# Key tiles spread by transfers, attention output in even rows, and one transfer per gate tile

## The chip, the cores and the metric

The kernel runs on one core of a Trainium2 chip. The metric is the device time of one execution in microseconds (us), as the median of several runs. The core's engines are named as in the profile: PE (TensorE matmuls), PEld (its weight loads), DVE (VectorE), ACT (ScalarE), POOL (GpSimd) and SP (SyncE, which here issues nearly all transfers, one after the other from one queue).

## The reference

128 sequences of 64 tokens with 128 channels go through four blocks, each with a condition vector of a sequence (`cond`) and a context of 64 tokens of a sequence (`ctx`). All arithmetic is float32. Cut to what matters here:

```python
# block L0 (and, with other weights, L2)
sh_sa, sc_sa, g_sa, sh_ff, sc_ff, g_ff = split(silu(t_emb) @ adaln_w + adaln_b, 6)
xm = ln(x) * (1 + sc_sa) + sh_sa
x = x + g_sa * (attend(q, k, v of xm @ qkv_w + qkv_b) @ sa_proj_w + sa_proj_b)   # self-attention
x = x + attend(ln(x) @ q_w + q_b, k and v of ctx) @ ca_proj_w + ca_proj_b        # cross-attention
x = x + g_ff * mlp(ln(x) * (1 + sc_ff) + sh_ff)
# block L1: cross-attention from a modulated x to a modulated context
# block L3: a small mixture of three experts with a gate
def attend(q, k, v):            # 16 heads of 8 channels
    return softmax(q @ k.T / sqrt(8)) @ v
```

## The kernel before, in words

The 8,192 tokens are 16 groups of 8 sequences (512 tokens). All of `x` stays in the on-chip memory, as 16 tiles `x0` to `x15` of 128 tokens by 4 by 128 channels. Five attention layers follow each other: L0s and L0c (self and cross of block L0), then the MLP of L0, then L1c, L2s and L2c, then the MLP of L2, then block L3.

In an attention layer a group goes through the generator `prepare` (load of the context, statistics, normalizing, transposing, then `kT`, `kbd`, `qT`, `vbd`), the two halves of `scores`, `turned` and `weighted`, and the generator `finish`. The function `step` writes by hand the order in which every engine gets its work: two steps for each group, with `go(prep, i + d)` and `go(fin, i - d)` taking the next part of a later or an earlier group. The order on each queue is exactly the order in which these lines issue. No scheduler changes it. `turned` follows `scores` by one step, and `weighted` by two.

Scores are matmuls over 32 rows, which are the 8 channels of 4 heads. To keep the heads apart, the keys stand in a block-diagonal tile `kbd` of 128 rows by 4 by 512: plane `j` holds the keys of one head of each four, and zeros in the other rows. POOL makes the four planes with four multiplications of `kT` by a column of a 0/1 `mask` (L444); DVE does it for the first group. `kbd` is drawn new from a pool for each group.

The values stand in `vbd`, two tiles that are kept, cleared once, with a column of ones for the softmax's sums. `weighted` gives `o`: in each 32 rows, rows 0 to 15 are the outputs of two heads and rows 16 and 17 the sums. There are two column planes, so that a second set of rows 0 to 15 belongs at rows 16 to 31 of the first plane.

`finish` divides. Part 1 writes the sums to DRAM by two transfers (`sums`, L538), reads them back spread over 128 rows (`rc`, L542), and moves the second plane's rows by four transfers `o<-o` (L545). Part 2 takes the reciprocal on DVE (L547), writes it back (`recs`, L549), loads the gate tile in a self-attention layer (`gt`, two transfers, L278) and loads the reciprocals spread over the rows (`rb`, L554). Part 3 multiplies on POOL (`oT`, L557) and adds the bias to `x`. Part 4 is the projection `py` on PE (L563).

`gt` has the gate and the gated bias of each token's sequence: 128 rows by 4 by 256. It is read from a DRAM table with one row of 1 KB for each sequence; every row is repeated for 64 tokens. It is loaded once a group in L0s and L2s, and once a group (a turn) in the MLP of L2.

Of the kernel before, what the change touches and what calls it, by code (L numbers as in the profile page):

```python
# [9 lines left out]
F32 = mybir.dt.float32  # L10
AF = mybir.ActivationFunctionType
ALU = mybir.AluOpType
# [23 lines left out]
for _name, _n in _VECS:  # L36
# [15 lines left out]
}  # L52
_RAW = [
    "x", "cond_1024", "ctx_1024", *_WTS,
    "L0_xcond_ca_proj_b", "L1_xcond_bp", "L2_xcond_b_cproj", "L3_xcond_router_b", "L3_xcond_e_b2",
# [4 lines left out]
def tile_kernel(ctx: ExitStack, tc: tile.TileContext, a: dict, out: bass.AP):  # L60
# [5 lines left out]
    def const(shape, name):  # L66
        return cp.tile(shape, F32, tag=name, name=name)
# [8 lines left out]
    nc.sync.dma_start(cond, a["cond_1024"])  # L76
    vec_rows = const([_NVEC, P], "vec_rows")
    nc.scalar.dma_start(vec_rows, a["vecs"])
    mask = const([P, 4], "mask")
    nc.scalar.dma_start(mask, a["mask"])  # L80

    w = {}

    def load_weights(prefix, pool=cp):
        for name, (k, n) in _WTS.items():
            if name.startswith(prefix):
                t = pool.tile([P, k, n], F32, tag=name, name=name)
                src = a[name]
                if len(src.shape) == 3:
                    src = src.rearrange("e c n -> (e c) n")  # L90
                nc.sync.dma_start(t, src.rearrange("(k p) n -> p k n", p=P))
                w[name] = t

    xs = [const([P, TT, P], f"x{s}") for s in range(NST)]
# [23 lines left out]

    ident = const([P, P], "ident")
    make_identity(nc, ident)  # L120
    nhalf = const([P, TT], "nhalf")
    G.memset(nhalf, -0.5)

# [37 lines left out]
    def mm(name):  # L161
        return pools[1].tile([P, 512], F32, tag="mm", name=name)
# [4 lines left out]
        Places.ak.tile([P, NB, 8, 32], F32, tag=f"vbd{i}", name=f"vbd{i}", bufs=1) for i in range(2)  # L167
    ]

    def clear(t):  # L170
        G.memset(t, 0.0)
        G.memset(t[0:L, :, :, 16:17], 1.0)
        G.memset(t[L:P, :, :, 17:18], 1.0)


# [2 lines left out]
    condT = const([P, P], "condT")  # L178
    scT = const([P, P], "scT")
    mods = {}  # L180

    def col(name, i=0):
        r = _ROW[name] + i
        return vec[:, r : r + 1]
# [19 lines left out]

    def folded_column(wp, bp, bv, i):
        pb = mm("pb")
        T.matmul(pb[:, 0:1], w[wp][:, 0], col(bv, i), start=True, stop=True)
        t = const([P, 1], "pb_" + wp)
        V.tensor_add(t, pb[:, 0:1], col(bp))
        proj_bias[wp] = t  # L210
# [3 lines left out]
    def gate_table(wmod, wp, i=2, bias=None):  # L214

        table = dp.tile([P, 2, P], F32, tag="gate_" + wp, name="gate_" + wp)
        rows = const([P, 2, P], "gate_rows")
        gb = const([P, P], "gate_bias")
        V.tensor_scalar_mul(gb, mods[wmod][:, i, :], proj_bias[wp] if bias is None else bias)

        def second():
            pg = mm("pg")
            for q, src in enumerate((mods[wmod][:, i, :], gb)):
                T.transpose(pg[:, ts(q, P)], src, ident)
            V.tensor_copy(rows, pg[:, 0 : 2 * P].rearrange("p (i c) -> p i c", i=2))
            nc.sync.dma_start(table, rows)
            gates[wp] = table

        return second

    def folded_row(wp, bp, bv):
        bvs = const([P, P], "bvs")
        V.tensor_copy(bvs, col(bv, 1).broadcast_to([P, P]))

        def second():
            pb = mm("pb")
            T.matmul(pb[:, :P], bvs, w[wp][:, 0], start=True, stop=True)
            V.tensor_add(row_bias[bp], row_bias[bp], pb[:, :P])
            proj_bias[wp] = row_bias[bp]

        return second

    def condition():
        pc = mm("pc")
        T.transpose(pc[:, :P], cond, ident)
        V.tensor_copy(condT, pc[:, :P])
        S.activation(scT, pc[:, :P], AF.Silu)
        pv = mm("pv")
        T.transpose(pv[:, :_NVEC], vec_rows, ident[:_NVEC, :_NVEC])
        V.tensor_copy(vec, pv[:, :_NVEC])  # L250
        V.tensor_scalar_add(vec1, vec, 1.0)

    first_mods = modulations("L0_xcond_adaln_w", "L0_xcond_adaln_b", 6, (1, 4))
# [19 lines left out]
    def gate_tile(pool, s, wp):  # L273

        gt = pool.tile([P, TT, 2, P], F32, tag="gt", name="gt")
        for h in range(2):
            r = gates[wp].rearrange("(s t h) i c -> s h t (i c)", t=TT, h=2)[s, h]
            nc.sync.dma_start(  # L278
                gt[ts(h, L)].rearrange("p t i c -> p t (i c)"),
                r.unsqueeze(0).broadcast_to([L, TT, 2 * P]),  # L280
            )
        return gt

    later_tables = [
# [14 lines left out]
    def by_batch(t):  # L299
        return t.rearrange("p (b l) -> p b l", b=NB)  # L300
# [80 lines left out]

    turn = [0]

    ctxT = dp.tile([NST, P, NT], F32, tag="ctxT", name="ctxT")

    def prepare(pools, at):
# [52 lines left out]
        i = turn[0] % 2  # L439
        turn[0] += 1  # L440
        vbd = vbds[i]
        kbd = pool.tile([P, 4, NB, L], F32, tag="kbd", name="kbd")
        for j in range(4):
            (V if at.get("first") else G).tensor_scalar(  # L444
                kbd[:, j], by_batch(kT), mask[:, j : j + 1], 1.0, ALU.mult, ALU.mult
            )
        yield
        pq = psum.tile([P, 512], F32, tag="mm", name="pq")
        T.matmul(pq, at["wq"], q_in, start=True, stop=True)  # L449
# [11 lines left out]
                    start=True, stop=True,  # L461
                )
        pv4 = pvv.rearrange("p b (i d) -> p b i d", d=HD)
        S.copy(vbd[0:L, :, :, 0:HD], pv4[0:L])
        S.copy(vbd[L:P, :, :, HD : 2 * HD], pv4[L:P])
        at["vbd"] = vbd

    def scores(pools, at, u):
# [61 lines left out]
    def finish(pools, at):  # L530

        pool, psum = pools[:2]
        s, o = at["s"], at["o"]
        cross = at["layer"][2] == "c"

        sums = dp.tile([16, NT], F32, tag="sums", name="sums", bufs=2)
        for j in range(2):
            nc.sync.dma_start(  # L538
                sums.rearrange("(g i j) t -> j g i t", i=2, j=2)[j], o[16 + j : P : 32, :, :]
            )  # L540
        rc = pool.tile([P, L], F32, tag="rc", name="rc")
        nc.sync.dma_start(rc, sums.rearrange("h (c t) -> (h c) t", t=L))  # L542

        for g in range(4):
            nc.sync.dma_start(o[32 * g + 16 : 32 * g + 32, 0, :], o[32 * g : 32 * g + 16, 1, :])  # L545
        yield
        V.reciprocal(rc, rc)  # L547
        recs = dp.tile([16, NT], F32, tag="recs", name="recs", bufs=2)
        nc.sync.dma_start(recs.rearrange("h (c t) -> (h c) t", t=L), rc)  # L549

        if not cross:
            gt = gate_tile(pool, s, at["wp"])
        rb = pool.tile([P, NT], F32, tag="rb", name="rb", bufs=1)
        nc.sync.dma_start(rb, recs.unsqueeze(1).broadcast_to([16, HD, NT]))  # L554
        yield
        oT = pool.tile([P, NT], F32, tag="oT", name="oT", bufs=1)
        G.tensor_tensor(oT, o[:, 0, :], rb, ALU.mult)  # L557
        bias = proj_bias[at["wp"]].unsqueeze(1).broadcast_to([P, TT, P]) if cross else gt[:, :, 1, :]
        G.tensor_tensor(xs[s], xs[s], bias, ALU.add)
        yield  # L560
        py = psum.tile([P, TT, P], F32, tag="mm", name="py")
        for t in range(TT):
            T.matmul(py[:, t, :], oT[:, ts(t, P)], w[at["wp"]][:, 0], start=True, stop=True)  # L563
        if cross:
            V.tensor_add(xs[s], xs[s], py)
        else:
            y = pool.tile([P, TT, P], F32, tag="y", name="y")
            V.tensor_tensor(y, py, gt[:, :, 0, :], ALU.mult)
            G.tensor_tensor(xs[s], xs[s], y, ALU.add)

    def attend(pools, ats):
# [5 lines left out]
        def go(gens, i):  # L577
            if 0 <= i < n:
                next(gens[i], None)
# [8 lines left out]
        def step(k, between=(), late=()):  # L588
# [11 lines left out]
            if past:  # L600
                weighted(pools, past["at"], past["u"], past["eT"])
            if u == 0:
                go(fin, i - 2)
                go(prep, i + 4)
                go(prep, i + 1)
                go(fin, i - 3)
            else:
                go(prep, i + 1)
# [16 lines left out]
    def attention_of(s, layer):  # L625
        if layer[2] == "s":
            wmod, wqkv, bqkv, wp = {
                "L0s": ("L0_xcond_adaln_w", "L0_xcond_qkv_w", "L0_xcond_qkv_b", "L0_xcond_sa_proj_w"),
                "L2s": ("L2_xcond_W_mod", "L2_xcond_W_qkv", "L2_xcond_b_qkv", "L2_xcond_W_proj"),
            }[layer]  # L630
            m = w[wqkv][:, 0]
            return dict(
                s=s, layer=layer, wmod=wmod, wp=wp, wq=m[:, 0:P], bq=col(bqkv, 0),
                wk=m[:, P : 2 * P], bk=col(bqkv, 1), wv=m[:, 2 * P : 3 * P],
            )
        wq, bq, wkv, bkv, wp = {
            "L0c": (
# [8 lines left out]
        }[layer]  # L646
        m = w[wkv][:, 0]
        return dict(
            s=s, layer=layer, wp=wp, wq=w[wq][:, 0], bq=col(bq), wk=m[:, 0:P], bk=col(bkv, 0),
            wv=m[:, P : 2 * P],  # L650
        )

# [537 lines left out]
    def stages():  # L1190
# [41 lines left out]
        clear(vbds[0])  # L1232
        ahead_1(0, 1, 2, 3)
        condition()
        ahead_1(0, 0)
        first_mods[0]()
        ahead_1(0, 0, 1, 2, 0, 0, 1)
# [11 lines left out]
            f()  # L1249
        first_mods[2]()  # L1250
        n = last + 2 + len(heads_0)
        for f in steps_1[6:-n]:
            f()
        for s in range(2):
            heads_0[3 + s] = lambda s=s, f=heads_0[3 + s]: (f(), load_context(s))
        rest = into_mlp(steps_1, heads_0, turns_0)
# [68 lines left out]
```

## Time and profile before

| what | value |
|---|---|
| median of 3 runs | 1628.25 us (1627.0 to 1634.33) |
| the profiled execution, its own time | 1626.31 us |
| its span, from the first instruction to the last | 1624.5 us |
| mean granted TensorE clock | 0.997 of full speed |
| POOL busy | 1072.5 us (66%) |
| time of all transfer packets on the main queue | 26.1% of 16 transfer engines' span |
| L0s, between starts of a group's first score reduction | 11.9 to 13.3 us |
| transfers that SP issues for a group in L0s | 11: `sums` 2, `rc` 1, `o` 4, `recs` 1, `gt` 2, `rb` 1 |

Busy times are of one profiled execution. In a line of the timeline the columns are the start, the time, the engine, the source line, the operation, what it writes and reads, and how often; in square brackets is how long the engine had stood idle before it, and what ended that. In a line of waits they are who waited, for whom, the sum in us, how often, and the longest. `SPq` is SP's queue: an issue there is not the transfer itself, which goes on after it.

### The profile page before, as it was taken

The page shows a single profiled execution, that of the slowest core. Times are in us where ns is not written, and L with a number is a line of the kernel's source. Part 1 is how long each engine was busy: PE and PEld are TensorE (multiplying, and loading weights), DVE is VectorE, ACT ScalarE, POOL GpSimd, SP SyncE. Part 2 cuts the span into 40 slices and gives each one's busy share as a digit, 9 for nine tenths or more (in the row PEclk, how much of TensorE's full clock was granted, in tenths as well). Part 3 has the DMA queues.
Part 4 walks back from the last instruction along what each step waited for, and adds up shares of the span by engine and source line. Part 5 has one row for each costly group of instructions (what it writes and reads, how often), then busy time and mean ns, then how long its engine had stood idle before and what let it go on. Part 6 is the DMA issues. An engine that isn't in the chain of part 4 may idle for free.

```text
span 1624.5 us, 64028 instructions
## 1 busy us (share of the span) xinstructions
PE 1573.8 (97%) x27842; PEld 1086.8 (67%) x27842; DVE 1240.4 (76%) x1566; ACT 1035.5 (64%) x1710; POOL 1072.5 (66%) x1786
## 2 busy tenths in 40 slices
PE   6999999998999899999999999998999999999998
PEld 4676777776544577776777777776777566666665
DVE  7898998898555688899899889896443566666666
ACT  5788777776433678878888888886334544444443
POOL 6687787766888789887787876775875333333322
PEclk9999999999999999999999999999999999999999
DMA  8334453332111022211334432222533111111100
GB/s 209 85 82 99 107 127 92 83 83 72 55 36 55 16 63 61 72 44 50 90 82 102 104 88 73 62 56 59 130 81 76 31 39 37 40 33 36 34 12 19
DMA packets 146775, 112.65 MB, mean 69 GB/s; under 512 B 36357, under 2 KB 125247, under 8 KB 146495
## 3 DMA queue, kind: packets, MB, share of 16 engines
q1 hardware_dynamic: 146288, 108.53, 26.1%
q8 instruction: 219, 3.59, 0.9%
q14 instruction: 61, 0.50, 0.1%
q10 hardware_dynamic: 207, 0.03, 0.0%
HBM read 83.99 MB, written 14.02 MB: 60 GB/s over the span
## 4 chain that ended last, share of the span: by engine, by line
PE 83%; DVE 12%; ACT 3%; issue 1%; DMA 0%; SPq 0%; DVEq 0%
PE sc L478 10%; PE pp L503 9%; PE po L520 7%; PE ph L693 7%; PE ph L1080 6%; PE ph L1081 6%; DVE e L487 6%; DVE mx L485 6%; PE po L1111 5%; PE psT L342 5%; PE pk L436 5%; PE py L563 4%; PE py L709 4%; PE py L699 3%; PE pvv L459 3%; PE pq L449 3%
## 5 line engine op out<-in xcount | busy, mean ns | idle before, releaser
L507 ACT ACTIVATE eT<-pp 128x1024 f32<-128x1024 f32 x320 | 329.7, 1030 | 160.8 <-PE pp L503 160.7
L485 DVE TENSOR_REDUCE mx<-sc 128x32 f32<-128x2048 f32 x160 | 366.6, 2291 | 83.6 <-PE sc L478 83.6
L487 DVE TENSOR_TENSOR e<-sc,mx 128x2048 f32<-128x2048 f32 x160 | 366.6, 2291 | 5.4
L503 PEld LDWEIGHTS pp<-ident,e 64*128 64x128 f32 x5120 | 183.9, 138 | 140.1 <-ACT eT L507 44.7
L503 PE MATMUL pp<-ident,e 64*128 64x64 f32 x5120 | 227.7, 229 | 7.2 <-DVE e L487 4.7
L444 POOL TENSOR_SCALAR kbd<-kT,mask 128x512 f32<-128x512 f32 x316 | 212.4, 690 | 31.3 <-ACT kT L438 28.3
L372 POOL TENSOR_SCALAR xn<-x,nmu,rs 128x128 f32<-128x128 f32 x508 | 223.6, 453 | 13.3
L557 POOL TENSOR_TENSOR oT<-o,rb 128x512 f32<-128x512 f32 x80 | 102.1, 1276 | 163.5 <-DMA rb<-recs 62.9
L478 PE MATMUL sc<-kbd,qT 32*64 32x256 f32 x5120 | 179.2, 387 | 16.6 <-DVE e L487 15.6
L694 ACT ACTIVATE h<-ph,vec 128x512 f32<-128x512 f32 x128 | 87.3, 687 | 149.9 <-PE ph L693 149.7
L520 PE MATMUL po<-eT,vbd 128*32 128x64 f32 x10240 | 178.1, 221 | 1.4 <-issue 1.3
L1087 ACT ACTIVATE h<-h 128x512 f32<-128x512 f32 x112 | 70.6, 630 | 149.8 <-DVE h L1083 130.9
L520 PEld LDWEIGHTS po<-eT,vbd 128*32 128x32 f32 x10240 | 151.3, 110 | 14.4 <-issue 2.0
L330 POOL TENSOR_TENSOR rs<-rs,nhalf 128x4 f32<-128x4 f32 x128 | 130.2, 1017 | 10.7
L478 PEld LDWEIGHTS sc<-kbd,qT 32*64 32x64 f32 x5120 | 97.7, 131 | 53.0 <-issue 19.6
L1083 DVE TENSOR_TENSOR h<-ph,ab 128x512 f32<-128x512 f32 x112 | 76.9, 687 | 62.6 <-PE ph L1081 62.5
L1116 DVE SCALAR_TENSOR_TENSOR acc<-po,pr,acc 128x128 f32<-128x128 f32 x192 | 67.2, 350 | 44.1 <-PE po L1111 39.6
L1080 PE MATMUL ph<-nx,w 128*128 128x512 f32 x192 | 100.7, 607 | 0.0
L528 ACT COPY o<-po 128x512 f32<-128x512 f32 x160 | 95.7, 598 | 5.1 <-PE po L520 2.0
L1081 PE MATMUL ph<-u,w_ev 128*128 128x512 f32 x192 | 98.9, 597 | 0.0
L1111 PEld LDWEIGHTS po<-w_2o,h 128*128 128x128 f32 x768 | 92.1, 192 | 8.7 <-issue 8.4
L1104 POOL TENSOR_SCALAR g<-g 128x512 f32<-128x512 f32 x16 | 9.9, 622 | 132.1 <-ACT g L1103 132.1
(259 smaller groups left out, 2868.5 us busy)
## 6 DMA issues: line engine op xcount, KB each, us to landing
rb<-recs SPq DMA_DIRECT2D x80, 256.0 KB
c<-in_ctx_dram SPq DMA_DIRECT2D x64, 256.0 KB
o<-o SPq DMA_DIRECT2D x320, 32.0 KB
gt<-gate_L_xcond_sa_proj_w SPq DMA_DIRECT2D x32, 256.0 KB
gt<-gate_L_xcond_W_proj SPq DMA_DIRECT2D x32, 256.0 KB
gt<-gate_L_xcond_W_mlp SPq DMA_DIRECT2D x32, 256.0 KB
x<-in_x_dram SPq DMA_DIRECT2D x16, 256.0 KB
ctxT<-cm SPq DMA_DIRECT2D x16, 256.0 KB
```

The source lines that it names most:

```text
L330: G.tensor_tensor(rs, rs, nhalf, ALU.pow)
L372: engine.tensor_scalar(xn[:, t, :], src[:, t, :], nmu[:, t : t + 1], rs[:, t : t + 1], ALU.add, ALU.mult)
L444: (V if at.get("first") else G).tensor_scalar(kbd[:, j], by_batch(kT), mask[:, j : j + 1], 1.0, ALU.mult, ALU.mult)
L478: T.matmul(sc[ts(h, L), g, ts(t2, 256)], qT[ts(g, 32), ts(b, L)], kbd[ts(g, 32), :, b, :], start=True, stop=True,)
L485: V.tensor_reduce(mx, sc.rearrange("p g (m k) -> p (g m) k", k=L), AX.X, ALU.max)
L487: V.tensor_tensor(e, sc.rearrange("p g (m k) -> p (g m) k", k=L), mx.unsqueeze(2).broadcast_to([P, 32, L]), ALU.subtract,)
L503: T.transpose(pp[:, h, ts(4 * g2 + 2 * i + t2, L)], e6[ts(h, L), 2 * gg + g2, t2, i], ident[ts(h, L), ts(h, L)],)
L507: S.activation(eT[:, gg], pp, AF.Exp, scale=HD ** -0.5)
L520: T.matmul(po[ts(g, 32), i, ts(2 * t2 + h, L)], at["vbd"][:, 4 * u + 2 * t2 + h, 2 * g + i, :], e7[:, g // 2, h, g % 2, i, t2, :], start=T ...
L1080: T.matmul(ps, wn, d["nx"], start=True, stop=False)
L1081: T.matmul(ps, we, d["u"], start=False, stop=True)
L1111: T.matmul(po[:, ex, :], d[q][:, ts(t, P)], k3["w_2o"][:, q, :], start=r == 0, stop=r == 1)
```

## The change

Four things are changed together.

1. The columns of the query and key weights are put in another order at run time (`reorder`), so that the rows of `kT` that belong to plane `j` are rows `j, j+4, j+8, ...`. Two `kbd` tiles are kept. The first two groups still fill them by the mask, which also writes the zeros; from the third group on, four transfers (`spread`) write only the key rows. `mask` is computed from the identity matrix.
2. The columns of `vbd` are laid out so that outputs stand in the even rows of `o` and sums in two odd rows. One transfer gives `sums`, one moves the second plane into the odd rows. The five projection weights are loaded with their rows in the matching order, by two transfers each, and `rb` is loaded by two transfers.
3. The gate table in DRAM is ordered so that the rows of a half of a group stand together, 4 KB, and `gt` is one transfer.
4. In `step`, `go(prep, i + 1)` (with the keys' transfers) stands ahead of `go(fin, i - 2)` (with `recs`). `finish` has one part more: `recs` is issued ahead of the context's load, `gt` and `rb` after it.

```diff
+    kbds = [
+        Places.ak.tile([P, 4, NB, L], F32, tag=f"kbd{i}", name=f"kbd{i}", bufs=1) for i in range(2)
+    ]
     def clear(t):
         G.memset(t, 0.0)
-        G.memset(t[0:L, :, :, 16:17], 1.0)
+        G.memset(t[0:L, :, :, 1:2], 1.0)
...
+    def reorder(engine, name, n):
+        for i in range(n):
+            t = const([P, P], "gate_bias")
+            cols = w[name][:, 0, ts(i, P)]
+            engine.tensor_copy(t.rearrange("p (g d j) -> p g d j", d=HD, j=4), by_element(cols))
+            engine.tensor_copy(cols, t)
...
         gt = pool.tile([P, TT, 2, P], F32, tag="gt", name="gt")
-        for h in range(2):
-            r = gates[wp].rearrange("(s t h) i c -> s h t (i c)", t=TT, h=2)[s, h]
-            nc.sync.dma_start(
-                gt[ts(h, L)].rearrange("p t i c -> p t (i c)"),
-                r.unsqueeze(0).broadcast_to([L, TT, 2 * P]),
-            )
+        r = gates[wp].rearrange("(s h t) i c -> s h (t i c)", t=TT, h=2)[s]
+        nc.sync.dma_start(
+            gt.rearrange("p t i c -> p (t i c)"),
+            r.unsqueeze(1).broadcast_to([2, L, TT * 2 * P]),
+        )
...
+    def spread(kbd, kT):
+        for j in range(4):
+            nc.sync.dma_start(kbd[j:P:4, j].rearrange("p b l -> p (b l)"), kT[j:P:4, :])
...
-        kbd = pool.tile([P, 4, NB, L], F32, tag="kbd", name="kbd")
-        for j in range(4):
-            (V if at.get("first") else G).tensor_scalar(
-                kbd[:, j], by_batch(kT), mask[:, j : j + 1], 1.0, ALU.mult, ALU.mult
-            )
+        kbd = kbds[i]
+        by_mask = turn[0] <= 2
+        if by_mask:
...
+        else:
+            spread(kbd, kT)
...
-        S.copy(vbd[0:L, :, :, 0:HD], pv4[0:L])
-        S.copy(vbd[L:P, :, :, HD : 2 * HD], pv4[L:P])
+        S.copy(vbd[0:L, :, :, 0 : 2 * HD : 2], pv4[0:L])
+        S.copy(vbd[L:P, :, :, 2 * HD : 4 * HD : 2], pv4[L:P])
...
-        for j in range(2):
-            nc.sync.dma_start(
-                sums.rearrange("(g i j) t -> j g i t", i=2, j=2)[j], o[16 + j : P : 32, :, :]
-            )
+        nc.sync.dma_start(sums.rearrange("(m i) t -> m i t", i=2), o[1:P:16, :, :])
...
-        for g in range(4):
-            nc.sync.dma_start(o[32 * g + 16 : 32 * g + 32, 0, :], o[32 * g : 32 * g + 16, 1, :])
+        nc.sync.dma_start(o[1:P:2, 0, :], o[0:P:2, 1, :])
         yield
         V.reciprocal(rc, rc)
         recs = dp.tile([16, NT], F32, tag="recs", name="recs", bufs=2)
         nc.sync.dma_start(recs.rearrange("h (c t) -> (h c) t", t=L), rc)
+        yield
         if not cross:
             gt = gate_tile(pool, s, at["wp"])
         rb = pool.tile([P, NT], F32, tag="rb", name="rb", bufs=1)
-        nc.sync.dma_start(rb, recs.unsqueeze(1).broadcast_to([16, HD, NT]))
+        for i in range(2):
+            r = recs.rearrange("(m i) t -> i m t", i=2)[i]
+            nc.sync.dma_start(rb[i:P:2, :], r.unsqueeze(1).broadcast_to([8, HD, NT]))
...
             if u == 0:
+                go(prep, i + 1)
                 go(fin, i - 2)
                 go(prep, i + 4)
-                go(prep, i + 1)
+                go(fin, i - 2)
                 go(fin, i - 3)
...
+        reorder(V, "L0_xcond_qkv_w", 2)
```

The remaining calls of `reorder` (eight pieces of the later layers' weights) run on POOL, one or two after every second step of layer L0s. In the changed kernel SP still issues 11 transfers for a group in L0s: `kbd` 4, `recs` 1, `gt` 1, `rb` 2, `sums` 1, `rc` 1, `o` 1.

More of the change, by code (lines that the diff above doesn't have):

```diff
@@ L52 @@
 }
+_TURNED = (
+    "L0_xcond_sa_proj_w", "L0_xcond_ca_proj_w", "L1_xcond_Wp", "L2_xcond_W_proj",
+    "L2_xcond_W_cproj",
+)
 _RAW = [
@@ L78, in tile_kernel @@
     nc.scalar.dma_start(vec_rows, a["vecs"])
-    mask = const([P, 4], "mask")
-    nc.scalar.dma_start(mask, a["mask"])
     w = {}
@@ L90, in load_weights @@
                     src = src.rearrange("e c n -> (e c) n")
-                nc.sync.dma_start(t, src.rearrange("(k p) n -> p k n", p=P))
+                if name in _TURNED:
+                    of = src.rearrange("(g i r) n -> i g r n", i=2, r=2 * HD)
+                    for i in range(2):
+                        nc.sync.dma_start(t[i:P:2, 0, :], of[i])
+                else:
+                    nc.sync.dma_start(t, src.rearrange("(k p) n -> p k n", p=P))
                 w[name] = t
@@ L120, in tile_kernel @@
     make_identity(nc, ident)
+    mask = const([P, 4], "mask")
+    V.tensor_reduce(mask, ident.rearrange("p (q j) -> p j q", j=4), AX.X, ALU.add)
     nhalf = const([P, TT], "nhalf")
@@ L180, in tile_kernel, with by_element, colp, colv @@
     mods = {}
+    vecp = const([P, _NVEC], "vecp")
+    vecv = const([P, _NVEC], "vecv")
+    def by_element(t):
+        return t.rearrange("p (g j d) -> p g d j", j=4, d=HD)
+    def colp(name, i=0):
+        r = _ROW[name] + i
+        return vecp[:, r : r + 1]
+    def colv(name, i=0):
+        r = _ROW[name] + i
+        return vecv[:, r : r + 1]
     def col(name, i=0):
@@ L206, in folded_column @@
         pb = mm("pb")
-        T.matmul(pb[:, 0:1], w[wp][:, 0], col(bv, i), start=True, stop=True)
+        T.matmul(pb[:, 0:1], w[wp][:, 0], colv(bv, i), start=True, stop=True)
         t = const([P, 1], "pb_" + wp)
@@ L225, in second @@
             V.tensor_copy(rows, pg[:, 0 : 2 * P].rearrange("p (i c) -> p i c", i=2))
-            nc.sync.dma_start(table, rows)
+            for h in range(2):
+                nc.sync.dma_start(
+                    table.rearrange("(s h t) i c -> h s t (i c)", t=TT, h=2)[h],
+                    rows[h:P:2].rearrange("p i c -> p (i c)"),
+                )
             gates[wp] = table
@@ L232, in folded_row @@
         bvs = const([P, P], "bvs")
-        V.tensor_copy(bvs, col(bv, 1).broadcast_to([P, P]))
+        V.tensor_copy(bvs, colv(bv, 1).broadcast_to([P, P]))
         def second():
@@ L241, in folded_row @@
         return second
-    def condition():
+    def reorder(engine, name, n):
[4 more added lines that the diff above has]
+            engine.tensor_copy(cols, t)
+    def condition():
+        vec_rows_p = const([P, P], "gate_bias")[:_NVEC]
+        vec_rows_v = const([P, 2, P], "gate_rows")[:_NVEC, 0, :]
+        V.tensor_copy(
+            vec_rows_p.rearrange("p (g d j) -> p g d j", d=HD, j=4), by_element(vec_rows)
+        )
+        V.tensor_copy(
+            vec_rows_v.rearrange("p (g r i) -> p g r i", r=2 * HD, i=2),
+            vec_rows.rearrange("p (g i r) -> p g r i", r=2 * HD, i=2),
+        )
         pc = mm("pc")
@@ L249, in condition @@
         T.transpose(pv[:, :_NVEC], vec_rows, ident[:_NVEC, :_NVEC])
+        T.transpose(pv[:, P : P + _NVEC], vec_rows_p, ident[:_NVEC, :_NVEC])
+        T.transpose(pv[:, 2 * P : 2 * P + _NVEC], vec_rows_v, ident[:_NVEC, :_NVEC])
         V.tensor_copy(vec, pv[:, :_NVEC])
+        V.tensor_copy(vecp, pv[:, P : P + _NVEC])
+        V.tensor_copy(vecv, pv[:, 2 * P : 2 * P + _NVEC])
         V.tensor_scalar_add(vec1, vec, 1.0)
@@ L275, in gate_tile @@
         gt = pool.tile([P, TT, 2, P], F32, tag="gt", name="gt")
-        for h in range(2):
-            r = gates[wp].rearrange("(s t h) i c -> s h t (i c)", t=TT, h=2)[s, h]
-            nc.sync.dma_start(
-                gt[ts(h, L)].rearrange("p t i c -> p t (i c)"),
-                r.unsqueeze(0).broadcast_to([L, TT, 2 * P]),
-            )
+        r = gates[wp].rearrange("(s h t) i c -> s h (t i c)", t=TT, h=2)[s]
+        nc.sync.dma_start(
+            gt.rearrange("p t i c -> p (t i c)"),
+            r.unsqueeze(1).broadcast_to([2, L, TT * 2 * P]),
+        )
         return gt
@@ L441, in prepare @@
         vbd = vbds[i]
-        kbd = pool.tile([P, 4, NB, L], F32, tag="kbd", name="kbd")
-        for j in range(4):
-            (V if at.get("first") else G).tensor_scalar(
-                kbd[:, j], by_batch(kT), mask[:, j : j + 1], 1.0, ALU.mult, ALU.mult
-            )
+        kbd = kbds[i]
+        by_mask = turn[0] <= 2
+        if by_mask:
+            for j in range(4):
+                (V if at.get("first") else G).tensor_scalar(
+                    kbd[:, j], by_batch(kT), mask[:, j : j + 1], 1.0, ALU.mult, ALU.mult
+                )
+        else:
+            spread(kbd, kT)
         yield
@@ L553, in finish @@
         rb = pool.tile([P, NT], F32, tag="rb", name="rb", bufs=1)
-        nc.sync.dma_start(rb, recs.unsqueeze(1).broadcast_to([16, HD, NT]))
+        for i in range(2):
+            r = recs.rearrange("(m i) t -> i m t", i=2)[i]
+            nc.sync.dma_start(rb[i:P:2, :], r.unsqueeze(1).broadcast_to([8, HD, NT]))
         yield
@@ L632, in attention_of @@
             return dict(
-                s=s, layer=layer, wmod=wmod, wp=wp, wq=m[:, 0:P], bq=col(bqkv, 0),
-                wk=m[:, P : 2 * P], bk=col(bqkv, 1), wv=m[:, 2 * P : 3 * P],
+                s=s, layer=layer, wmod=wmod, wp=wp, wq=m[:, 0:P], bq=colp(bqkv, 0),
+                wk=m[:, P : 2 * P], bk=colp(bqkv, 1), wv=m[:, 2 * P : 3 * P],
             )
@@ L648, in attention_of @@
         return dict(
-            s=s, layer=layer, wp=wp, wq=w[wq][:, 0], bq=col(bq), wk=m[:, 0:P], bk=col(bkv, 0),
+            s=s, layer=layer, wp=wp, wq=w[wq][:, 0], bq=colp(bq), wk=m[:, 0:P], bk=colp(bkv, 0),
             wv=m[:, P : 2 * P],
@@ L1251, in stages @@
         n = last + 2 + len(heads_0)
-        for f in steps_1[6:-n]:
-            f()
+        names = (
+            ("L0_xcond_q_w", 1), ("L0_xcond_kv_w", 1), ("L1_xcond_Wq", 1), ("L1_xcond_Wkv", 1),
+            ("L2_xcond_W_qkv", 2), ("L2_xcond_W_qc", 1), ("L2_xcond_W_kvc", 1),
+        )
+        for i, f in enumerate(steps_1[6:-n]):
+            f()
+            if i % 2 and i // 2 < len(names):
+                reorder(G, *names[i // 2])
         for s in range(2):
```

## The prediction

> **What bounds the kernel now.** I read the page's first part and its chain, then the waits of TensorE's weight loads and of the transfer queue, then the timeline of one self-attention group, and at last the trace's records of semaphores and packets. The page (busy time, then the chain by engine, then the group of instructions that the change mostly removes):
>
> ```profile
> PE 1573.8 (97%) x27842; PEld 1086.8 (67%) x27842; DVE 1240.4 (76%) x1566; ACT 1035.5 (64%) x1710; POOL 1072.5 (66%) x1786
> ...
> PE 83%; DVE 12%; ACT 3%; issue 1%; DMA 0%; SPq 0%; DVEq 0%
> ...
> L444 POOL TENSOR_SCALAR kbd<-kT,mask 128x512 f32<-128x512 f32 x316 | 212.4, 690 | 31.3 <-ACT kT L438 28.3
> ```
>
> TensorE is the bound; POOL has a third of the span free and is not on the chain at all. By the starts of the score reductions (L485) a group of attention takes 12.0 us in all five layers. The waits:
>
> ```profile
> PEld py L563 <- POOL oT L557: 13.9, 22, 1.6
> ...
> PEld py L563 <- POOL x L559: 7.6, 13, 0.6
> ```
>
> ```profile
> SPq L549 <- DVE rc L547: 137.7, 77, 3.4
> SPq L542 <- DMA sums<-o: 131.2, 86, 3.4
> SPq L554 <- DMA recs<-rc: 81.3, 58, 3.0
> ```
>
> All that TensorE waits for POOL in the attention's tail is 13.9 + 7.6 = 21.5 us. SP, which issues every transfer in order, stops three times a group: for the sums, the reciprocal, and its landing. One self-attention group in the timeline:
>
> ```profile
> 208.65 1.16 SPq L538 DMA_DIRECT2D sums<-o  x2
> ...
> 211.38 0.32 SPq L542 DMA_DIRECT2D rc<-sums  x1
> 211.75 2.96 SPq L545 DMA_DIRECT2D o<-o  x4
> ...
> 213.13 0.69 ACT L438 ACTIVATE kT<-pk,vec 128x512 f32<-128x512 f32 x1 [0.40 <-PE pk L436]
> ...
> 215.19 2.69 POOL L444 TENSOR_SCALAR kbd<-kT,mask 128x512 f32<-128x512 f32 x4
> ...
> 215.57 0.33 SPq L549 DMA_DIRECT2D recs<-rc  x1
> ...
> 215.94 2.08 SPq L278 DMA_DIRECT2D gt<-gate_L_xcond_sa_proj_w  x2
> ...
> 218.71 0.54 SPq L554 DMA_DIRECT2D rb<-recs  x1
> ...
> 222.41 1.27 POOL L557 TENSOR_TENSOR oT<-o,rb 128x512 f32<-128x512 f32 x1 [1.29 <-DMA rb<-recs]
> ```
>
> The reader should see the order sums, rc, o, recs, gt, rb, next sums, and that oT starts when rb has landed, behind gt's bytes. SP still has spare time in the 12 us.
>
> **The gate tile: from sixteen engines to two.** Today gt is two transfers, each with 64 as outermost count on both sides. The trace's semaphore records show how far a transfer is spread: gt, o, rb and rc each raise their semaphore sixteen times, sums (outermost counts 8 and 4) five times, the 54 rows of vec_rows ten times, a 3-row load four, a 1-row load twice. One early update comes from the issuer when fewer than sixteen engines work, so the engines are 16, 4, 9, 3 and 1: the largest number up to 16 that divides both outermost counts. The new gt has 128 rows outermost in its target and 2 in its source (2 x 64 repeats x 4 KB). No transfer of this trace has a 2 there, so the bounds are 2 engines (by the rule in sums and vec_rows) and 16 (as gt now). I take 2.
>
> The Trainium skill, page "DMA: Bandwidth & Descriptors", section "Rules for kernel authors", speaks against this edit: an outermost count below 16 confines the whole transfer to at most that many engines. The same section also says that two transfers to disjoint halves of the partitions should be one; by that advice alone the sum would be the first rival's 1618 us, by the other it is the forecast's.
>
> Packet durations in this trace: 512 B 27 ns, 1,024 B 46, 2,048 B 84 (undisturbed; mean 121), 3,072 B 121 (mean 141). That is 37.5 ns per KB and 9 ns, so an estimated 159 ns for 4 KB; scaled by 141/121 it could be 185. Each of two engines moves 64 of them: 10.2 us (up to 11.8). Today's 2 x 16 packets of 1 KB cost each engine 1.5 us. The same page's section "Specifications" gives about 27 GiB/s for an engine, which would make it 9.0 us and the final sum about 55 us less; the packets measured here decide.
>
> **What the slow gate tile holds up.** The queue's packets go out in order on each engine: rb, behind gt, lands 3.3 to 5.9 us after its issue in the self layers, but 3.0 to 4.3 in the first two cross layers. In the new order SP issues four kbd, recs, gt, two rb, sums, rc, o. rb has outermost counts 64 and 8, so eight engines; sums 8 and 8, eight. I take it that these include gt's two. From gt's issue: first packet after 1.3 us (today 1.4 median), 10.2 of gt, 2 x 8 x 0.084 = 1.3 of rb, 0.2 of sums, 0.7 to land: 13.7 us. Only then can SP issue rc (0.32), o (0.6), four kbd (0.59 each, as the 16-row o transfers), recs (0.33), with gaps 0.35: 4.0 us, and the next gt follows. The reciprocal fits beside the kbd issues (rc lands 1.5 us after its issue at best). The loop is 17.7 us against 12.0.
>
> It reaches TensorE twice: sc waits for kbd, and py, which stands in the middle of TensorE's step, waits for oT, which waits for rb. 5.7 us in each of 32 self-attention groups (L0s, L2s): **+182 us**. In the last four groups of each, c (32 packets of 512 B) goes out between recs and gt: about 1 us each, **+8**.
>
> In the last MLP each turn loads a gt. A turn is now (1263.3 - 1141.1)/15 = 8.1 us by L719; with two buffers the transfers can run back to back, so it becomes 10.2: 16 x 2.1 = **+33**.
>
> **Keys by transfers.** 78 groups lose four POOL instructions of 0.69 us: 215 us by that product, about the page's 212 for 79 (group 0's are on DVE). It is hidden work: oT follows rb or xm on POOL, not kbd, so I take 0 of the 21.5 us. The transfers of four times 32 rows of 2 KB go to sixteen engines, 8 packets each, 0.7 us. Their wait for kT now stands ahead of recs on SP. In a cross group the score matmul starts at 640.43 and kT ends at 645.01; the issues end near 647.6, so recs goes out 0.9 later than its 646.76 and rb lands near 652.7, with c ahead of it and only eight engines. oT starts at 654.57: 1.9 us spare, cost 0 (bounds: 0, and 1 us times 48 if that cover is gone). kbd lands near 649.2; scores of the next group start at 652.69: 3.5 spare, as long as SP is free when kT is done. That fails behind the slow gt, and is in the loop already.
>
> **Edits with one answer.** One transfer for o in place of four and one sums in place of two save 1.8 and 0.6 us of SP's issues, which give the four kbd their room. The strided ACT copies into vbd keep their element count: 0. POOL's sixteen 128x128 copies for the later weights, at most 0.45 us each by L372's row, go into the time that kbd left. At the start DVE reorders qkv_w before the first statistics: they start at 4.69, qkv_w lands at 2.19 + 4.05 = 6.24, and four copies of some 0.25 us follow: **+2.6**. Instruction order on TensorE and ACT is otherwise the same.
>
> **Sum.** 182 + 8 + 33 + 2.6 = 226 us on the profiled execution's 1626.3 us (span 1624.5 and 1.8 around it), so 1852; that execution is 1.9 below the runs' median, and I say 1852.
>
> **Rivals.**
> *The gate tile is spread after all.* Sixteen engines with 8 packets of 4 KB each: 1.3 us, less than now; SP's loop fits into 12 us. Then the gain is what py no longer waits, 0 to 21.5 us, against 2.6 at the start: 1607 to 1629, say 1618. For it: today's gt is spread. Against: the five updates of sums. 9 in 100, split between faster and same.
> *gt on two engines, but sums not queued behind it.* The issue records name eight semaphores in turn, and a transfer waits for the one eight before it, so the third kbd waits for gt's landing anyway: 12.5 us after issue, then two kbd, recs and gaps, 14.2 a group. 32 x 2.2 + 8 + 33 + 2.6 = 114: 1740. At the lowest, 13.0 us of packets on those engines a group: 32 + 33 + 3 = 68, so 1694. 22 in 100.
> *Keys late without the gate's help.* From 3.5 us of hold-up on SP the scores wait in every layer; 0.5 us in each of 78 groups would give 1665. Nothing in the profile holds SP so long at kT. 2 in 100.
>
> **How the numbers follow.** Forecast 67 in 100. Its own range: 185 ns packets add 1.66 us to 48 tiles, 80 us, to 1932, and 18 of the 48 us of the cross layers, to 1950; below, a loop shorter by 1 us (no gaps, and a landing of 0.3 us) is 32 us less, 1820. Taking in the second rival, 1700 to 1950. About 0.5% (8 us) is what can be told from no change. Slower 0.91, same 0.05, faster 0.04.
>
> **What would show it.** Right: gt raising its semaphore three times and rb nine; self groups near 17.7 us and cross groups still 12.0; SP's wait for sums at some 10 us a group; TensorE idle ahead of py and sc in L0s and L2s; MLP turns over 10 us; POOL about 205 us less busy. Wrong: gt landing within 5 us of its issue, or self groups at 12 us; if cross groups are longer than 12.5, I have underrated the wait for kT.

## The result, and the profile after

The changed kernel takes **1926.44 us** (median of 4 runs, 1921.41 to 1931.35) against 1628.39 us for the kernel before on the same chip (4 runs, 1627.0 to 1634.33). The ratio is 1.182, 95% interval 1.178 to 1.186: slower by 298 us. The profiled execution took 1921.41 us, its span is 1919.6, and its mean granted TensorE clock 0.941.

The page of the changed kernel: busy time by engine, the granted clock in 40 slices, and the chain by engine and by line:

```profile
PE 1662.5 (87%) x27844; PEld 1142.3 (60%) x27844; DVE 1248.7 (65%) x1575; ACT 1052.2 (55%) x1710; POOL 869.4 (45%) x1490
...
PEclk9888888999999999999788888999989989999999
...
PE 47%; DMA 30%; POOL 9%; ACT 5%; issue 3%; SPq 3%; DVE 3%; POOLq 0%; DVEq 0%; ACTq 0%
DMA rb<-recs 19%; PE ph L1145 5%; PE pp L568 5%; PE ph L1146 5%; DMA gt<-gate_L_xcond_W_mlp 5%; PE po L1176 4%; PE sc L543 4%; DMA sums<-o 3%; PE po L585 3%; PE ph L758 3%; PE py L627 3%; DMA recs<-rc 3%; PE py L764 3%; POOL oT L621 3%; PE psT L397 3%
```

POOL lost 203 us of work, and nothing came of it: transfers, 0% of the chain before, are 30% now, and `rb` alone is 19%. The clock's digits fall to 8 and 7 in the two self-attention layers and are 9 in most other slices.

The waits of the changed kernel (who waits, for whom, sum in us, times, longest), first the compute engines', then SP's:

```profile
POOL oT L621 <- DMA rb<-recs: 462.8, 49, 18.2
...
PEld py L627 <- POOL oT L621: 223.0, 64, 9.0
...
DVE y L784 <- DMA gt<-gate_L_xcond_W_mlp: 89.7, 14, 11.6
```

```profile
SPq L604 <- DMA sums<-o: 407.2, 80, 11.5
```

SP's wait for the sums was 131.2 us before. One loop of SP in L0s, from the timeline of the changed kernel:

```profile
202.64 0.58 SPq L333 DMA_DIRECT2D gt<-gate_L_xcond_sa_proj_w  x1
...
203.76 1.26 SPq L618 DMA_DIRECT2D rb<-recs  x2
...
207.71 0.59 SPq L602 DMA_DIRECT2D sums<-o  x1
...
216.97 0.32 SPq L604 DMA_DIRECT2D rc<-sums  x1
217.00 1.26 POOL L621 TENSOR_TENSOR oT<-o,rb 128x512 f32<-128x512 f32 x1 [10.87 <-DMA rb<-recs]
...
217.34 0.53 SPq L606 DMA_DIRECT2D o<-o  x1
...
217.97 2.45 SPq L443 DMA_DIRECT2D kbd<-kT  x4
...
218.32 2.06 PE L627 MATMUL py<-L_xcond_sa_proj_w,oT 128*128 128x128 f32 x8 [4.34 <-POOL oT L621]
...
220.52 0.53 SPq L610 DMA_DIRECT2D recs<-rc  x1
221.09 0.58 SPq L333 DMA_DIRECT2D gt<-gate_L_xcond_sa_proj_w  x1
```

`gt` is issued at 202.64. The sums, a small transfer issued 5.07 us later, have landed only at 216.97, 14.33 us after `gt`'s issue; `oT` starts in the same instant, after POOL had stood 10.87 us for `rb`. Then come `rc`, `o`, four `kbd` and `recs`, and the next `gt` goes out 4.12 us after the sums.

Where the time went, by the starts of the score reductions and of the gate's use in the last MLP (us; "left out" is 1624.5 or 1919.6 less the rows above it):

| stage | before | after | difference |
|---|---|---|---|
| start, to the first score reduction | 16.9 | 19.2 | +2.3 |
| L0s, the 16 groups whose loop has a `gt` in it | 191.5 | 307.5 | +116.0 |
| L2s, the same 16 groups | 193.4 | 303.5 | +110.1 |
| MLP of L2, first to last use of `gt` | 122.2 | 173.6 | +51.4 |
| L1c | 194.6 | 200.5 | +5.9 |
| left out (most of it L0c, L2c, the other MLP and L3) | 905.9 | 915.3 | +9.4 |

### The profile page after: what moved, and what is told of

Read it like the earlier page. It is cut to its first block, busy times and chain, and to the rows that moved or that the text cites. A ratio compares the mean times of both kernels' runs of the same rounds, so it can differ in the third digit from the quotient of the medians.

```text
span 1919.6 us, 63825 instructions
## 1 busy us (share of the span) xinstructions
PE 1662.5 (87%) x27844; PEld 1142.3 (60%) x27844; DVE 1248.7 (65%) x1575; ACT 1052.2 (55%) x1710; POOL 869.4 (45%) x1490
## 4 chain that ended last, share of the span: by engine, by line
PE 47%; DMA 30%; POOL 9%; ACT 5%; issue 3%; SPq 3%; DVE 3%; POOLq 0%; DVEq 0%; ACTq 0%
DMA rb<-recs 19%; PE ph L1145 5%; PE pp L568 5%; PE ph L1146 5%; DMA gt<-gate_L_xcond_W_mlp 5%; PE po L1176 4%; PE sc L543 4%; DMA sums<-o 3%; PE po L585 3%; PE ph L758 3%; PE py L627 3%; DMA recs<-rc 3%; PE py L764 3%; POOL oT L621 3%; PE psT L397 3%
## 5 line engine op out<-in xcount | busy, mean ns | idle before, releaser
L568 PEld LDWEIGHTS pp<-ident,e 64*128 64x128 f32 x5120 | 196.5, 147 | 146.8 <-issue 38.8
L568 PE MATMUL pp<-ident,e 64*128 64x64 f32 x5120 | 241.9, 239 | 7.0 <-DVE e L552 4.5
L427 POOL TENSOR_SCALAR xn<-x,nmu,rs 128x128 f32<-128x128 f32 x508 | 223.7, 453 | 13.2
L543 PE MATMUL sc<-kbd,qT 32*64 32x256 f32 x5120 | 192.8, 411 | 17.4 <-ACT eT L572 8.8
L543 PEld LDWEIGHTS sc<-kbd,qT 32*64 32x64 f32 x5120 | 103.0, 141 | 62.6 <-issue 27.0
L608 DVE RECIPROCAL rc<-rc 128x64 f32<-128x64 f32 x80 | 43.8, 547 | 125.7 <-DMA rc<-sums 125.6
L627 PE MATMUL py<-L_xcond_sa_proj_w,oT 128*128 128x128 f32 x128 | 32.8, 437 | 82.4 <-POOL oT L621 82.4
```

Of the source, the lines that this page charges most:

```text
L427: engine.tensor_scalar(xn[:, t, :], src[:, t, :], nmu[:, t : t + 1], rs[:, t : t + 1], ALU.add, ALU.mult)
L543: T.matmul(sc[ts(h, L), g, ts(t2, 256)], qT[ts(g, 32), ts(b, L)], kbd[ts(g, 32), :, b, :], start=True, stop=True,)
L568: T.transpose(pp[:, h, ts(4 * g2 + 2 * i + t2, L)], e6[ts(h, L), 2 * gg + g2, t2, i], ident[ts(h, L), ts(h, L)],)
```

## Experiments

The first theory was that of the prediction: one transfer with an outermost count of 2 sits on two transfer engines, and everything that shares these in order waits behind it. Rivals were that one transfer for 128 rows is slow as such, that TensorE's lower clock is the cause, and that the keys' transfers cost something too. Each ratio is to the kernel before, with its 95% interval.

**Mend the gate alone.** The changed kernel, with `gt` as two transfers with 64 outermost:

```diff
-        nc.sync.dma_start(gt.rearrange("p t i c -> p (t i c)"),
-            r.unsqueeze(1).broadcast_to([2, L, TT * 2 * P]))
+        for h in range(2):
+            nc.sync.dma_start(gt[ts(h, L)].rearrange("p t i c -> p (t i c)"),
+                r[h].unsqueeze(0).broadcast_to([L, TT * 2 * P]))
```

> The changed kernel with the gate tile loaded by two transfers again, each with 64 repeats outermost, so on sixteen engines; all else as changed. Theory (the gate tile on two engines and what queues behind it is the whole loss): self-attention groups back at 12.0 us, turns of the last MLP at 8.1, 1610 to 1650 us in all. Rival (the keys' transfers ahead of the reciprocals on SP, or rb on eight engines, cause a large part): over 1700 us, self groups of 14 us or more.

Measured: 1661.67 us, ratio 1.0206 [1.016, 1.0251]. 265 of the 298 us are gone with the same bytes, the same 4 KB packets, and one transfer more. The last MLP is back at 122.2 us. But 33 us stay, 12 more than the expectation's upper end, and all but the start's 2.6 of them the prediction had put at nothing.

**Break the gate alone, in the kernel before.** Only the table's order (its two writes are left out of the diff here) and the single transfer are put into it.

```diff
-        for h in range(2):
-            r = gates[wp].rearrange("(s t h) i c -> s h t (i c)", t=TT, h=2)[s, h]
-            nc.sync.dma_start(gt[ts(h, L)]..., r.unsqueeze(0).broadcast_to([L, TT, 2 * P]))
+        r = gates[wp].rearrange("(s h t) i c -> s h (t i c)", t=TT, h=2)[s]
+        nc.sync.dma_start(gt..., r.unsqueeze(1).broadcast_to([2, L, TT * 2 * P]))
```

> The kernel before with the gate tile alone in one transfer from the reordered table; keys, o, sums and rb as before. Theory: the loop is gt's 13.9 us until the sums have landed (rb takes half the time on sixteen engines), then rc 0.3, four o 2.4, recs 0.3 and gaps, 17.3 to 18.3 us a self group; with 48 us in the last MLP some 1860, between 1830 and 1900. Rival (other parts are needed for the loss): under 1700.

Measured: 1891.71 us, 1.1617 [1.1595, 1.164]. Here too `gt` raises its semaphore three times and lands 13.35 us after its issue (median in L0s). From both sides the gate tile is the change's main cost. The changed kernel is still 35 us slower than this one, so the other parts of the change cost something beside the slow gate too.

**One transfer on more engines.** The table's rows are written more than once, so that one transfer can have 4 or 16 as the source's outermost count.

```diff
-            r.unsqueeze(1).broadcast_to([2, L, TT * 2 * P]),
+            r.unsqueeze(1).broadcast_to([4, L // 2, TT * 2 * P]),    # rows written twice
+            r.unsqueeze(1).broadcast_to([16, L // 8, TT * 2 * P]),   # rows written eight times
```

> The changed kernel with a gate table that holds every row block twice, so that the one transfer's source has 4 outermost: same bytes and packets, four engines. Theory: gt raises its semaphore five times, its packets take 5.4 us in place of 10.8, the self group's loop falls from 18.8 to some 13.4, turns of the MLP are at 8.1 again: 1640 to 1690. If the loss does not go with the engines (packets of 4 KB, or one semaphore for 512 KB), it stays over 1850.

> As before with eight copies of every row block: one transfer, sixteen engines, 8 packets of 4 KB on each. Theory: within 1% of the kernel with two transfers for the gate tile, 1610 to 1650, up to 20 us of it for the sixteen writes of each table; the semaphore is raised sixteen times. Rival: one large transfer is itself slow, over 1700.

Measured: with 4 the semaphore is raised five times, `gt` lands in 8.1 to 8.6 us in the self-attention layers (medians), and the kernel takes 1737.74 us, 1.0679 [1.0654, 1.0703]. With 16 there are sixteen updates, landing in 5.1 to 5.5 us, and 1669.56 us, 1.0253 [1.0227, 1.0279], of which about 10 us are the additional table writes (groups 0 to 3 of L0s take 49.1 us, and 38.2 with two transfers; the 16 writes of a table occupy SP for 12.0 us there). That is within 1% of the kernel with two transfers, as expected, but above the 1650 us named with it. So one transfer as such is not slow; the time follows the outermost count. The size for 4 was missed: most of its self-attention groups go by turns at 12 to 13.5 and at 16 to 18.5 us, not all at 13.4. Landing times of 12.9, 8.4 and 5 us do not turn into time in proportion.

The Trainium skill, page "DMA: Bandwidth & Descriptors", section "Rules for kernel authors", says that an outermost count below 16 confines a transfer to at most that many engines, and that two transfers to disjoint halves of the partitions should rather be one. The runs agree with the first (2, 4 and 16 gave two, four and sixteen engines); against the second, for a transfer like this one, the two halves took 1661.67 us and the one transfer with 2 outermost 1926.44.

**Is it TensorE?** Three more matmuls of 512 columns ahead of `py` in each self-attention group:

```diff
+        if not cross:
+            for _ in range(3):
+                T.matmul(py.rearrange("p t c -> p (t c)"), ident,
+                         w["L0_xcond_adaln_w"][:, 0, 0:512], start=True, stop=True)
```

> The changed kernel (one gate transfer on two engines), with three extra 512-column matmuls ahead of the projection in every self-attention group, whose result is overwritten: some 1.1 us each by the row of pk, 3.4 us in 32 groups, 108 us of added TensorE work. Theory (the loop of the self groups runs through SP and the transfers, and TensorE waits in it, at half its clock or not): 1920 to 1945. If TensorE's own time, with its lower clock after each wait, is on that loop: 1980 or more.

Measured: 1923.05 us, 1.1796 [1.1758, 1.1834], not longer than without them. TensorE was busy for 64.8 us more, and the clock rose to 0.954. The waits of this kernel show the same two ends of the loop, on SP and on POOL:

```profile
SPq L604 <- DMA sums<-o: 422.0, 80, 11.7
```

```profile
POOL oT L621 <- DMA rb<-recs: 469.8, 50, 17.9
```

So TensorE has room ahead of `py` in these groups, and its lower clock goes with the waits and is not their cause.

**Take `gt` off SP's queue.** If only the order in one queue mattered, another queue would help much:

```diff
-        nc.sync.dma_start(gt...
+        nc.scalar.dma_start(gt...
```

> The changed kernel with the one gate transfer (two engines) issued from ACT's queue instead of SP's. If rb and sums are late because they stand in the same queue behind gt on its two engines, they pass it now: rb lands within 7 us of its issue, sums within 4. gt itself still needs 11 us and more, so the self group is bounded by some 13.5 us of packets on those engines, and POOL and DVE wait for gt: 1740 to 1820 in all. If the two engines' load alone sets the time, no change: 1900 or more.

Measured: 1881.78 us, 1.1544 [1.1521, 1.1567]; missed, it helps little. SP's waits in this kernel:

```profile
SPq L604 <- DMA sums<-o: 224.8, 80, 7.7
SPq L618 <- DMA recs<-rc: 173.4, 80, 6.6
```

The sums come back sooner (224.8 us instead of 407.2), and in L0s `rb` lands in 3.9 us in the median instead of 12.4. Now the small transfers that pass while `gt` runs are late: in L0s `recs` lands in 4.6 us instead of 1.6 and `kbd` in 5.6 instead of 1.9. The packet records do not name the engine, but while `gt` runs its 4 KB packets follow each other in two rows, and between two of a row stands one small packet of SP's queue. So a transfer of several small packets waits for a 4 KB one between each. What costs is that two engines are busy for so long; a queue of its own moves the lateness to other transfers. The same page, section "Queues, rings and completion order", has the engines going in turn over the queues that have work for them, a packet at a time; the records here show such turns, one of 4 KB at a time.

**The 33 us left: which part of the change?** The mended kernel, with the keys made by the mask on POOL again and all else as changed:

```diff
-        by_mask = turn[0] <= 2
+        by_mask = True
```

> The changed kernel with the gate tile by two transfers on sixteen engines, and with the keys of every group made by the mask on POOL again (in the two kept tiles); even rows of o, two rb transfers on eight engines and the order of the steps stay changed. Theory for the 34 us that are left with the gate mended (the four key transfers, issued ahead of recs, gt and rb on SP, make rb late): these go, 1615 to 1635. Rival (rb in two transfers on eight engines is what is late): still 1650 or more.

Measured: 1631.58 us (10 runs), 1.0012 [1.0, 1.0024]. So outputs in even rows, `rb` on eight engines, the new weights' order and the new order of a step cost and gain nothing together that can be told apart; the keys by transfers cost the 30 us. Of these the gate groups of L0s and L2s have 11 and 10 (203.6 us against 192.5, and 204.8 against 194.3), and L1c, a cross-attention layer, has nothing (197.4 against 196.9). The timelines of the two kernels show where. First the mended one with transfers, in the longest group of its L0s (16.0 us), then the one with the mask, in an ordinary group of L0s (12.0 us):

```profile
147.33 3.22 SPq L444 DMA_DIRECT2D kbd<-kT  x4
...
148.34 0.54 DVE L609 RECIPROCAL rc<-rc 128x64 f32<-128x64 f32 x1
...
150.66 0.52 SPq L611 DMA_DIRECT2D recs<-rc  x1
...
159.72 1.26 POOL L622 TENSOR_TENSOR oT<-o,rb 128x512 f32<-128x512 f32 x1 [6.82 <-DMA rb<-recs]
...
161.03 2.08 PE L628 MATMUL py<-L_xcond_sa_proj_w,oT 128*128 128x128 f32 x8 [2.54 <-POOL oT L622]
```

```profile
169.51 0.54 DVE L609 RECIPROCAL rc<-rc 128x64 f32<-128x64 f32 x1
...
170.08 0.33 SPq L611 DMA_DIRECT2D recs<-rc  x1
...
177.30 1.28 POOL L622 TENSOR_TENSOR oT<-o,rb 128x512 f32<-128x512 f32 x1 [2.09 <-DMA rb<-recs]
...
179.37 1.08 PE L628 MATMUL py<-L_xcond_sa_proj_w,oT 128*128 128x128 f32 x8
```

With the mask `recs` goes out 0.57 us after the reciprocal's start, with the transfers 2.32, because SP is still issuing keys; `oT` follows 7.8 and 11.4 us after the reciprocal. In the first fence `py` stands 2.54 us for `oT`, in the second it does not. The medians over the gate groups of L0s are closer than these two groups: 0.57 and 1.77 us for `recs`, 7.5 and 9.2 us for `oT`.

**Is it the keys' landing, or what they hold up?** The mask makes the keys, and SP issues the four transfers all the same, into memory that nobody reads, for groups 7 to 64 (`by_mask = True` as before):

```diff
+        if 6 < turn[0] <= 64:
+            for j in range(4):
+                nc.sync.dma_start(w["L0_xcond_adaln_w"][j:P:4, 0, 0:NT], kT[j:P:4, :])
```

> Keys made by the mask on POOL, as in the version with two gate transfers that takes 1631.6 us; but SP also issues, at the keys' old place, four transfers of kT's rows (32 rows of 2 KB each) into a piece of memory that nobody reads, for groups 7 to 64. So SP's four issues, their wait for kT and their bytes are all there, and no score matmul waits for them. Theory A (what costs some 30 us is that SP's queue, held by kT and four issues, sends recs and rb later, so that oT and py are late): most of the cost comes back, the 16 gate groups of L0s at 200 us or more against 192.5, in all 1645 to 1662. Theory B (what costs is the landing of kbd itself ahead of the scores): 1628 to 1638, as without the transfers.

Measured: 1661.7 us, 1.0186 [1.0137, 1.0236]; the gate groups of L0s take 204.2 us, against 203.6 with the keys in use and 192.5 without the transfers. In L2s it is half of the loss, 199.7 against 204.8 and 194.3. No score matmul waits for these copies, so in L0s the landing of `kbd` is not what costs: it is SP's four issues, with their wait for `kT`, and the bytes. The waits of this kernel, for `rb` and then of the projection for `oT`, and the latter in the kernel with the keys in use:

```profile
POOL oT L623 <- DMA rb<-recs: 140.9, 49, 7.8
...
PEld py L629 <- POOL oT L623: 55.7, 52, 3.5
```

```profile
PEld py L628 <- POOL oT L622: 61.8, 55, 3.8
```

`oT`'s wait was 107.3 us with the mask alone and 198.7 with the keys in use. The projection's was 16.8 us with the mask alone; the copies bring nearly all of it back, without a score that waits.

**Issues or bytes?** The keys' transfers from POOL's queue, and from ACT's:

```diff
-            nc.sync.dma_start(kbd[j:P:4, j]...
+            nc.gpsimd.dma_start(kbd[j:P:4, j]...     # or nc.scalar
```

> The gate tile by two transfers; the four key transfers issued from POOL's queue, at the place where POOL made the keys by the mask. If the 34 us that the keys cost are SP's 2.4 us of issues ahead of recs, gt and rb, they go: 1625 to 1640, and rb lands before oT needs it. If they are the keys' bytes on the sixteen engines, ahead of rb's, it stays at 1655 or more.

> As with POOL's queue, but the four key transfers are issued by ACT right after it has written kT. SP is free as well, but ACT, which stands before the exponentials, loses some 2 us of a 12 us group: 1635 to 1680; if ACT's issues hide too, 1625 to 1640; if the bytes cost, 1655 or more, with rb landing as late as from SP.

Measured: from POOL 1652.48 us, 1.0146 [1.0124, 1.0168], between the two expectations. L1c is as in the kernel before (194.7 us), but the gate groups of L0s still take 204.7. They do so by another wait. `recs` goes out 0.57 us after the reciprocal's start again, and the projection waits 24.2 us for `oT` instead of 61.8. But in L0s POOL issues the first key transfer 1.1 us after `kT` (SP 0.03), a transfer lands 3.5 us after its issue (1.9), all four 7.7 us after `kT` (4.5; medians), and now scores wait for them:

```profile
PE sc L544 <- DMA kbd<-kT: 16.3, 13, 2.4
```

So the projection's wait came for the most part from the issues on SP. How much of the 30 us is bytes stays open: from POOL's queue the keys also go in packets of 4 KB, not 2. From ACT it is 1764.59 us, 1.0836 [1.0816, 1.0855]; missed by 85 us. The waits and the timeline of that kernel show why:

```profile
ACT eT L573 <- DMA kbd<-kT: 184.3, 68, 3.7
```

```profile
203.57 2.41 ACTq L444 DMA_DIRECT2D kbd<-kT  x4
...
206.03 1.02 ACT L573 ACTIVATE eT<-pp 128x1024 f32<-128x1024 f32 x1 [2.48 <-DMA kbd<-kT]
```

The four issues take 2.41 us of ACT, and the exponentials stand right behind them, in every layer (L1c is 222.8 us). An issue is work on its engine like any other.

**The order of the step.** With the gate mended, `recs` ahead of the keys; and then the whole order of before (`recs`, `gt`, `rb`, then the keys):

```diff
             if u == 0:
-                go(prep, i + 1)
                 go(fin, i - 2)
+                go(prep, i + 1)
                 go(prep, i + 4)
                 go(fin, i - 2)
```

```diff
             if u == 0:
-                go(prep, i + 1)
                 go(fin, i - 2)
-                go(prep, i + 4)
                 go(fin, i - 2)
+                go(prep, i + 4)
+                go(prep, i + 1)
```

> The gate tile by two transfers, the keys by transfers, but the first part of the reciprocals (recs) ahead of the keys in the step; gt and rb stay behind them. If what costs is recs waiting for kT and for the keys' issue, most of the 34 us goes: 1625 to 1640. If it is the 2.4 us of key issues ahead of gt and rb wherever recs stands, it stays at 1650 to 1665.

> The gate tile by two transfers, and the order of before: recs, gt and rb ahead of the keys' transfers. rb is then as early as before, and oT no longer waits for it; but in a self group the keys are issued some 11 us after the group's first score matmul, and land when the next group's scores start. Theory: TensorE waits for keys in place of py, 1645 to 1700. Rival (the keys still have time): 1630 to 1640.

Measured: 1694.2 us, 1.0382 [1.0347, 1.0417], and 1852.72 us, 1.1372 [1.1338, 1.1405]. Both are slower than keys first (1661.67), by 32 and by 191 us; both missed upward, since the first was expected at 1665 at most and the second at 1700. In the first, SP waits 203.9 us for DVE's reciprocal with the keys behind it. The waits of the second, on TensorE and on SP:

```profile
PE sc L544 <- DMA kbd<-kT: 173.4, 73, 5.2
```

```profile
SPq L611 <- DVE rc L609: 389.2, 80, 6.4
```

SP stands for the reciprocal with the keys queued behind it, and now the scores do wait for `kbd`, in every layer (L1c is 236.1 us). Of the three orders run with the keys' transfers on SP, keys ahead of the reciprocals, as the change has it, costs least.

## Why the prediction was right, and where not

- *Sixteen engines to two:* right. `gt` raises its semaphore three times, `rb` and `sums` nine, `kbd` and `o` sixteen.
- *Packets of 4 KB at 159 ns:* the median is 159 ns; the mean is 170, which on 64 packets is 10.9 us rather than 10.2.
- *The loop of 17.7 us:* the mechanism was right, the size short. Sums landed 13.9 to 15.4 us after `gt`'s issue, 14.4 in the median (13.7 predicted), and what follows took 4.1 to 5.4 us, 4.6 in the median (4.0). By the table a group takes 307.5/16 = 19.2 and 303.5/16 = 19.0 us. The 32 groups cost 226 us, where 182 + 8 = 190 were predicted. This is the largest mis-sized term, 36 us.
- *Sums queued behind `gt`:* right, and with it the rival of 1740 us fell: SP waits 407.2 us for them.
- *The last MLP:* 51.4 us for 33. The turns after the fourth took 10.0 to 11.2 us, about the 10.2 predicted, but for one of 13.2, which waited for the projection. The first four took 13.8, 14.9, 11.7 and 16.1, 15.7 more than four of 10.2: there the queue still carries the last `rb` of L2c and the weights of L3, behind the same `gt`. The prediction took a steady loop for all sixteen turns.
- *Keys by transfers, at 0:* wrong, and this is the step that failed. With the gate mended they cost 30 us. In the changed kernel their share is not known: no run has the slow gate and the keys by the mask. The table leaves about 15 us beyond the terms above; but the kernel before with the slow gate alone is 35 us faster than the changed one, so part of the 36 us in the loop may be theirs as well. The prediction looked at a cross-attention group, where it found 1.9 us to spare, and at `kbd` as what could be late. For L1c this held, 197.4 us against 196.9. (In the changed kernel the cross groups took 12.2 to 12.5 us, up to the 12.5 that it had named as the sign of an underrated wait for `kT`.) The loss shows most in the self-attention groups, where `gt` also stands ahead of `rb`, and the experiment with copies that nobody reads shows that it is `recs` and `rb` behind the keys' issues that are late. The rival "keys late" named 1665 us, near the mended kernel's 1661.67, but through scores waiting for keys, which is not how it came.
- *POOL:* 203 us less, as said (205), and worth nothing, as said.
- *The start:* 2.3 us, 2.6 predicted.
- *The rival that the gate is spread after all* named 1618 us and would have been a gain. With sixteen engines the kernel takes 1661.67: even then the change would have been slower.

In sum 226.1 + 51.4 + 2.3 + 15.3 = 295.1 us of span are found, against 226 predicted; the missing 69 are 36 in the loop, 18 in the MLP, and 15 in the last. That 1926 us still lies inside the range is in part luck: its upper end, 1950, was set by packets of 185 ns, and they took 170 in the mean. What filled the rest of the room were the MLP's first turns and the parts put at nothing.

The loop also offers a reason for the odd time with four engines: a wait that just exceeds 12 us shifts the order of transfers for the next group. That was only argued. No version run here beats the kernel before; the best is the change with the gate mended and the keys by the mask, 1.0012 [1.0, 1.0024].

## What to carry to other kernels

When two transfers become one, look at the outermost counts of both sides, and count the semaphore's updates in the trace: fewer engines cost every transfer that shares them, in the same queue or another. Work taken from an engine that is not on the chain was worth nothing here, but the issues put in its place stand in a queue that may be: name each instruction that goes out behind them (here `recs` and `rb`), for each kind of group apart. The slack of a loop must be worked out in the stage with the longest loop, not in a neighbouring one.

## What the runs showed of the hardware

The granted clock fell in the very groups that waited for transfers. Three windows of the changed kernel: inside the gate groups of L0s (57 to 365 us), about those of L2s (905 to 1209 us), and most of L2c with the start of the last MLP (start and end, length, busy times of PE, PEld, DVE, ACT and POOL, clock, transfer share, GB/s):

```profile
100.00:292.00 192.00, 138.40 (x3062) 100.19 (x3050) 113.98 (x82) 100.70 (x177) 73.11 (x114) 0.87 0.22 75
...
950.00:1255.00 305.00, 238.07 (x5376) 171.09 (x5378) 192.26 (x140) 180.05 (x300) 120.34 (x180) 0.88 0.23 78
1255.00:1400.00 145.00, 139.76 (x3067) 102.45 (x3064) 106.99 (x90) 100.36 (x149) 69.08 (x107) 0.98 0.23 72
```

In the clock's records the rate is one half in 41 stretches of the changed kernel, of 3.4, 6.8 or (three of them) 10.2 us, against three stretches before; 37 of the 41 begin in or just after a stretch of more than 2.5 us in which TensorE stood idle. `py` then takes 2.06 us instead of 1.08, and TensorE's busy time rose by 89 us with two instructions more. The Trainium skill, page "TensorE: Matmul & The Clock Gate", section "What's actually happening", knows just these two rates and a window of about 3.4 us, and the stretches here fit it. In the self-attention groups it seems to have cost little: with the added matmuls the clock in L0s's gate groups was 0.90 instead of 0.86, and they took 305.4 us instead of 307.5.

The four engines' case was the other surprise: half the load on each engine, and yet 76 us slower than sixteen.
